# Copies of the gram's blocks on GpSimd, written as products with ones

## The chip, the cores and the metric

The kernel runs on one core of a Trainium2 chip. The metric is device time in microseconds: the median of three runs of the kernel before is 2724.28 us (2723.8 to 2724.82). The core's engines are named in the profile as PE (TensorE matmul) and PEld (its weight loads), DVE (VectorE), ACT (ScalarE), POOL (GpSimd) and SP (SyncE, which only issues DMAs here). They run side by side and wait for each other by semaphores; each executes its own instructions in program order. An instruction that waits holds up everything behind it on its engine.

## The reference, cut to what matters

Eight images of 768 channels and 32x32 pixels pass through two layers, each `x = x + layer(groupnorm(x))`. Layer 0 is an attention whose scores are made of the variances of keys and values. Layer 1 is a 1x1 convolution over the normalised image and 28 correlation channels: the normalised pixel times its neighbours at 28 offsets of a 7x7 window.

```python
def _L1_conv_ref(feature, conv_w, conv_b):
    norm = jnp.sqrt(jnp.sum(feature * feature, axis=1, keepdims=True))
    feat_n = feature / jnp.maximum(norm, EPS)
    feat_pad = jnp.pad(feat_n, ((0, 0), (0, 0), (PAD, PAD), (PAD, PAD)))
    corr = jnp.stack([jnp.sum(feat_pad[:, :, r:h + r, cc:w + cc] * feat_n, axis=1) for r, cc in _offsets()], axis=1)
    x = jnp.concatenate([feature, corr], axis=1)
    out = jnp.einsum('bchw,oc->bohw', x, conv_w) + conv_b[None, :, None, None]
    return out
...
x = x + _L0_conv_ref(_gn(x), L0_conv_W_qkv, L0_conv_W_proj, L0_conv_b_proj)
x = x + _L1_conv_ref(_gn(x), L1_conv_conv_w, L1_conv_conv_b)
```

## The kernel before

All arithmetic is fp32. An image lies on the chip as 128 partitions by 6 channel chunks by 1024 pixels. The large products (keys and values, projection, convolution) use a scheme with seven block products in place of eight; the sums of blocks that it needs for keys and values are made on GpSimd: `make_sums` (lines 584 to 590), eight products or sums of 128x384 (`s`) for each pair of token groups. These are TENSOR_TENSOR instructions.

The order of the work on every engine is written out when the program is built. A planner (`Clock`) keeps an estimated time; jobs get due times with `later.after(...)` and are issued when the estimate reaches them; TensorE's units (a gram, one block product, four steps of attention) are taken from hand-written lists. The estimates fix only the order of instructions; on the chip semaphores alone decide when each starts.

In the main loop, layer 1 of image b-1 runs beside the second half of keys and values and the attention of image b. The attention of a pair of heads goes over 8 key blocks: ScalarE makes the exponentials `ex` (line 721) and, for some pairs, sums of exponentials `junk` (line 731), TensorE multiplies them with the values (`av`, line 746), and ScalarE copies `av` out.

The correlations of layer 1 (class `Corr`) are made from grams. The image `f` has 8 blocks of 128 pixels (4 rows of 32).

- `turn(t)` copies block t into a tile `turn`, in two instructions, the left and the right half of the rows apart (line 1065), each of 128x384 elements in runs of 16. The pool `turnpool` has one buffer. For the last image ScalarE makes these copies (`act_copy`), for the seven others GpSimd.
- `gram(t)` (24 matmuls, line 1080, into `gr`) multiplies the block with the rows about it, and then issues `turn(t + 1)`, which must wait until the gram has read the one buffer. Later VectorE copies `gr` into `win`, and SP stores it.
- After four grams, `diagonals` reads back the wanted diagonals as `dd`. `scale` takes the squared norms `m` on VectorE and raises them to the power -1/2 on GpSimd (`rn`, line 1125, a TENSOR_TENSOR with `ALU.pow`). Five VectorE instructions make `dn` from `dd` and `rn`; TensorE transposes it (`ct`, line 1136), VectorE copies the result to `cr`, and SP stores it. When both halves of the image are stored, `gather` fetches the correlation channels, which the convolution's last units use.

In TensorE's order, the first `ct` of an image stands between 24 and 8 of the 32 `av` matmuls of four attention steps, behind gram 4 and ahead of gram 5 (in the first image, ahead of gram 6 and behind the `av`). On GpSimd, the first `rn` stands behind `turn` 5 and ahead of `turn` 6. `turn` 0 of the images from the second on is issued ahead, between two `make_sums`.

GpSimd has one more kind of work: `spread` takes the largest key variance over all partitions (`most`, line 661, PARTITION_ALL_REDUCE), once for each half of each image's heads. In images two to seven, the one for the first half comes between `turn` 0 and `turn` 1. Instructions named MODIFY_POOL_CONFIG, which are not in the kernel's text, stand before each of these reductions and before some of the products that follow them.

`ones` is a constant tile of 128x64 ones (line 392), there for the attention's column sums. `windows(ap, dims...)` makes a view with steps written out by hand, each as (step, count).

Of the kernel before, what the change touches and what calls it, by code (L numbers as in the profile page):

```python
# [8 lines left out]
ALU = mybir.AluOpType  # L9
# [7 lines left out]
J = C // P  # L17
# [11 lines left out]
HW = W // 2  # L29
# [42 lines left out]
def windows(ap, *dims):  # L72

    return bass.AP(tensor=ap.tensor, offset=ap.offset, ap=[list(d) for d in dims])
# [83 lines left out]
def two_layers(ctx, tc, x, wkv, wproj, bproj, wconv, wcorr, bconv, out):  # L158
    nc = tc.nc
# [53 lines left out]
    def act_copy(us, to, at):  # L213
        nc.scalar.copy(to, at)  # L214
        clock.act = max(clock.act, clock.now) + us
# [175 lines left out]
    ones = const.tile([P, HD], F32, name="ones")  # L391
# [14 lines left out]
    rows = [dconst.tile([NROW, ROW], F32, name=f"rows{i}") for i in range(2)]  # L406
# [642 lines left out]
    class Corr:  # L1049
# [3 lines left out]
        def turn(self, t):  # L1053

            last = self.b == NB - 1
            pl, tag = (expool, "ex") if last else (turnpool, "turn")
            flat = pl.tile([P, N if last else J * P], F32, tag=tag, name=f"turn{self.b}_{t}")[:, : J * P]
            self.turned[t] = flat.rearrange("p (j s m) -> p j s m", j=J, s=2)
            to = flat.rearrange("p (j s y x) -> p j s y x", j=J, s=2, x=HW)
            rows = self.f[:, :, t * P : (t + 1) * P].rearrange("p j (y s x) -> p j y s x", y=4, s=2)  # L1060
            for side in range(2):
                if last:
                    act_copy(0.5, to[:, :, side], rows[:, :, :, side, :])
                else:
                    nc.gpsimd.tensor_copy(to[:, :, side], rows[:, :, :, side, :])  # L1065

        def gram(self, t):

# [440 lines left out]
```

## Time and profile before

The profiled execution took 2723.3 us, of which the core's span in the trace is 2721.6 us; the rest lies around it. TensorE's mean granted clock is 0.992 of full speed.

| | us busy | instructions |
|---|---|---|
| TensorE matmuls | 2649.8 | 9831 |
| VectorE | 1632.4 | 4160 |
| ScalarE | 1365.4 | 1841 |
| GpSimd | 355.3 | 442 |
| of GpSimd: the four lines of `make_sums` | 262.3 | 256 |
| of GpSimd: copies `turn` | 54.5 | 112 |
| of GpSimd: `rn` | 16.5 | 16 |
| of GpSimd: `most` | 6.9 | 16 |

How to read the views. A line of the groups has line, engine, operation, tile written and tile read, count, busy us and mean ns of one, and then the idle time of the engine just before these instructions, with what ended it. A line of the waits has the engine and tile that waited, what it waited for, the us in total, the number of waits and the longest; "issue" stands where the profile shows nothing that was waited for. A line of the view in order of time has start, length, engine, line, operation, tiles and count, and in brackets the idle time before it and its releaser. PEclk is the granted share of TensorE's full clock. Queue entries ("POOLq") are instructions of the engine's sequencer, which are not counted as busy.

### The profile page before, as it was taken

What the parts mean: (1) busy time and instruction counts of PE and PEld (TensorE: products, weight loads), DVE (VectorE), ACT (ScalarE), POOL (GpSimd) and SP (SyncE); (2) the same over time, 40 slices, a digit from 0 to 9 for tenths busy, and PEclk for the clock granted to TensorE, in tenths of its full rate; (3) what the DMA queues carried; (4) which work ended last, traced back from release to release, by engine and by line L of the source; (5) the groups of instructions that cost most, each with busy time, mean ns of one, the idle gap of its engine ahead of it and who ended that gap; (6) DMA issues with size and microseconds to landing.
All of it is one profiled execution on the core that took longest, in us unless ns stands there. A gap on an engine that the chain in (4) does not pass through costs nothing.

```text
span 2721.6 us, 30651 instructions
## 1 busy us (share of the span) xinstructions
PE 2649.8 (97%) x9831; PEld 1230.9 (45%) x9831; DVE 1632.4 (60%) x4160; ACT 1365.4 (50%) x1841; POOL 355.3 (13%) x442
## 2 busy tenths in 40 slices
PE   7999999999999999999999999999999999999999
PEld 4443454345543454434544345443454434544344
DVE  5859734775347853478524875258742587525864
ACT  1497078700697006970079701796017960189600
POOL 4220120003200032000320012200122001220000
PEclk9999999999999999999999999999999999999999
DMA  7764456354553645626556365462654626545243
GB/s 275 297 233 134 142 191 179 105 201 154 158 180 112 205 152 157 194 90 210 158 153 191 92 208 167 141 205 79 223 167 139 189 82 230 172 116 158 86 127 101
DMA packets 323355, 446.04 MB, mean 164 GB/s; under 512 B 59458, under 2 KB 245170, under 8 KB 323194
## 3 DMA queue, kind: packets, MB, share of 16 engines
q1 hardware_dynamic: 321962, 441.32, 50.9%
q10 hardware_dynamic: 1232, 2.75, 0.3%
q8 instruction: 79, 1.29, 0.2%
q14 instruction: 82, 0.67, 0.1%
HBM read 377.49 MB, written 64.40 MB: 162 GB/s over the span
## 4 chain that ended last, share of the span: by engine, by line
PE 89%; DMA 5%; issue 3%; DVE 2%; ACT 1%; POOL 1%; SPq 0%; DVEq 0%; POOLq 0%; ACTq 0%
PE x L359 35%; PE av L746 22%; PE y L359 17%; PE z L359 9%; PE gr L1080 3%; DMA x<-x1d 1%; DMA di<-ir 1%; PE den L779 1%; DMA rd<-di 1%; PE x L988 1%; PE den L829 1%; PE y L988 1%; DMA vdr<-rsv 1%; PE z L988 1%; ACT ex L721 0%
## 5 line engine op out<-in xcount | busy, mean ns | idle before, releaser
L721 ACT ACTIVATE ex<-bc,nk 128x1024 f32<-128x1024 f32 x768 | 826.8, 1137 | 449.1 <-DMA bc<-vdr 227.0
L746 PE MATMUL av<-ex,v 128*64 128x512 f32 x3072 | 705.3, 604 | 4.8 <-ACT ex L721 4.6
L731 ACT ACTIVATE junk<-bk,vm 128x1024 bf16<-128x1024 f32 x368 | 420.4, 1142 | 42.1 <-DMA bk<-kdr 22.8
L746 PEld LDWEIGHTS av<-ex,v 128*64 128x64 f32 x3072 | 230.5, 138 | 442.7 <-issue 380.1
L152 DVE TENSOR_TENSOR acc<-acc,ex 128x1024 f32<-128x1024 f32 x350 | 402.0, 1215 | 0.0
L214 ACT COPY kp<-x 128x384 f32<-128x384 f32 x28 | 13.4, 478 | 559.2 <-PE x L359 559.2
L359 PE MATMUL y<-kv,s 128*128 128x384 f32 x744 | 260.7, 491 | 0.0
L359 PE MATMUL x<-kv,xn 128*128 128x384 f32 x756 | 257.1, 490 | 2.8 <-DVE xn L152 1.6
L359 PE MATMUL x<-kv,s 128*128 128x384 f32 x744 | 254.3, 489 | 0.0
L359 PEld LDWEIGHTS x<-kv,xn 128*128 128x128 f32 x756 | 144.1, 191 | 106.0 <-issue 7.1
L359 PEld LDWEIGHTS x<-kv,s 128*128 128x128 f32 x744 | 138.7, 190 | 101.9 <-issue 9.1
L359 PEld LDWEIGHTS y<-kv,s 128*128 128x128 f32 x744 | 137.8, 190 | 94.8 <-issue 7.3
L480 POOL TENSOR_TENSOR rstda<-vea,neghalf 128x1 f32<-128x1 f32 x8 | 4.8, 595 | 1009.9 <-DVE vea L152 1009.9
L359 PE MATMUL x<-v,wt 128*128 128x512 f32 x288 | 130.2, 596 | 0.0
L359 PE MATMUL z<-kv,xn 128*128 128x384 f32 x372 | 126.9, 488 | 0.0
L152 DVE TENSOR_TENSOR v<-y,v 128x128 f32<-128x128 f32 x180 | 40.9, 282 | 137.5 <-PE y L359 137.5
L359 PE MATMUL x<-f,wt 128*128 128x512 f32 x252 | 116.2, 601 | 1.9 <-DVE x L152 1.8
L584 POOL TENSOR_TENSOR s<-xn 128x384 f32<-128x384 f32 x64 | 68.0, 1070 | 290.2 <-PE x L359 202.2
L152 DVE BATCH_NORM_STATS2 vbn<-v 128x6 f32<-128x64 f32 x720 | 101.8, 211 | 0.0
L152 DVE COPY win<-gr 128x133 f32<-128x133 f32 x64 | 18.4, 288 | 128.2 <-PE gr L1080 118.6
L1065 POOL COPY turn<-f 128x384 f32<-128x384 f32 x112 | 54.5, 514 | 305.4 <-PE gr L1080 292.2
L152 DVE SCALAR_TENSOR_TENSOR x<-x,bconv_sb,x 128x512 f32<-128x512 f32 x63 | 45.8, 746 | 78.1 <-DMA x<-x1d 55.9
(191 smaller groups left out, 3040.3 us busy)
## 6 DMA issues: line engine op xcount, KB each, us to landing
kv<-kvs SPq DMA_DIRECT2D x124, 576.0 KB
kv<-in_wkv_dram SPq DMA_DIRECT2D x95, 576.0 KB
bc<-vdr SPq DMA_DIRECT2D x96, 512.0 KB
f<-in_x_dram SPq DMA_DIRECT2D x48, 512.0 KB
bk<-kdr SPq DMA_DIRECT2D x46, 512.0 KB
x1d<-f SPq DMA_DIRECT2D x42, 512.0 KB
x<-x1d SPq DMA_DIRECT2D x42, 512.0 KB
out_dram<-x SPq DMA_DIRECT2D x82, 256.0 KB
```

Source lines behind the costliest of these rows:

```text
L152: return getattr(self.engine, name)(*args, **kw)
L214: nc.scalar.copy(to, at)
L359: nc.tensor.matmul(t, lhsT=lhsT, rhs=rhs, start=p in FIRST and k == 0, stop=stop and k == len(pairs) - 1, skip_group_check=True,)
L584: nc.gpsimd.tensor_tensor(self.sums[g][:, 0], a[g][2], a[g][3], ALU.add)
L721: nc.scalar.activation(ex, self.bc[e], AF.Exp, scale=self.kv.nk[self.half][:, h, t : t + 1])
L731: nc.scalar.activation(junk, self.bk[e], AF.Exp, scale=self.kv.m2[self.half][:, h, t : t + 1], accum_out=self.sums[:, e, t : t + 1],)
L746: nc.tensor.matmul(self.av[e * HD : (e + 1) * HD, hf, :], lhsT=self.vt[:, t, e, :], rhs=exs[e][:, hf * HF : (hf + 1) * HF], start=t == 0, ...
L779: nc.tensor.matmul(den[at * 32 : (at + 1) * 32, :], lhsT=ones[:, 0:32], rhs=self.acc[e][:, hf * HF : (hf + 1) * HF], start=True, stop=True,)
L829: nc.tensor.matmul(den[e * HD : (e + 1) * HD, :], lhsT=ones, rhs=self.acc[e][:, at], start=True, stop=True)
L988: nc.tensor.matmul(t, lhsT=wcorr_sb[at, i, :], rhs=cs[at, tokens, :], start=False, stop=True, skip_group_check=True)
L1065: nc.gpsimd.tensor_copy(to[:, :, side], rows[:, :, :, side, :])
L1080: nc.tensor.matmul(ps[side * HD : (side + 1) * HD, :n].rearrange("p (y x) -> p y x", x=WIDE), lhsT=block[:, j, side, :], rhs=image[:, 4 * ...
```

## The change

The two GpSimd copies of a `turn` become products of the same block with ones. The second operand is a view of the tile `ones` in which the 6 channel chunks have step 0, the 4 rows a step of 16 and the 16 pixels a step of 1, so that it has the shape of the block. The last image's `turn`, on ScalarE, stays as it is.

```diff
@@ -1062,7 +1062,8 @@
                 if last:
                     act_copy(0.5, to[:, :, side], rows[:, :, :, side, :])
                 else:
-                    nc.gpsimd.tensor_copy(to[:, :, side], rows[:, :, :, side, :])
+                    half = rows[:, :, :, side, :]
+                    nc.gpsimd.tensor_tensor(to[:, :, side], half, windows(ones, ones.ap[0], (0, J), (HW, 4), (1, HW)), ALU.mult)
```

Lines behind it are one higher in the changed kernel: `rn` is line 1126 there, `ct` 1137, the gram 1081.

## The prediction

> **What bounds the kernel now.** I read the page first, then the waits of TensorE, VectorE and GpSimd, then each of these engines in order of time around the longest waits.
>
> ```profile
> PE 2649.8 (97%) x9831; PEld 1230.9 (45%) x9831; DVE 1632.4 (60%) x4160; ACT 1365.4 (50%) x1841; POOL 355.3 (13%) x442
> ...
> L584 POOL TENSOR_TENSOR s<-xn 128x384 f32<-128x384 f32 x64 | 68.0, 1070 | 290.2 <-PE x L359 202.2
> ...
> L1065 POOL COPY turn<-f 128x384 f32<-128x384 f32 x112 | 54.5, 514 | 305.4 <-PE gr L1080 292.2
> ```
>
> TensorE has work for 97% of the span; GpSimd, whose instructions change, for 13%. A saving can only come from TensorE's 72 us without work (2721.6 - 2649.8) or from slow matmuls. The last two lines are the prices: a product of 128x384 takes twice a copy of the same size. Next the waits, from one answer for all engines: us in total, times, longest.
>
> ```profile
> DVE dn L152 <- POOL rn L1125: 57.4, 8, 9.7
> ...
> POOL rn L1125 <- issue: 45.5, 6, 8.2
> ...
> PE ct L1136 <- DVE dn L152: 33.4, 6, 6.2
> ```
>
> Nearly half of TensorE's idle time is one wait, six times: the transpose `ct` of the normalised diagonals waits for `dn`, VectorE for `rn`, and GpSimd, six times, waits before `rn` for nothing that the profile names. The view of line 1125 names what stands there:
>
> ```profile
> L1125 POOLq MODIFY_POOL_CONFIG  x12: 11/11/11, 722.6 to 2400.7; - x12
> ```
>
> Two such instructions precede each of the six `rn`, one for each image from the second to the seventh that goes through layer 1 beside the next image's attention. GpSimd in order of time in the first of these six:
>
> ```profile
> 683.90 0.43 POOL L661 PARTITION_ALL_REDUCE most<-top  x1 [7.43 <-DVE top L152]
> 688.71 0.95 POOL L1065 COPY turn<-f 128x384 f32<-128x384 f32 x2 [4.37 <-PE gr L1080]
> ...
> 721.59 0.96 POOL L1065 COPY turn<-f 128x384 f32<-128x384 f32 x2 [8.49 <-PE gr L1080]
> 730.46 1.05 POOL L1125 TENSOR_TENSOR rn<-m,neghalf 128x4 f32<-128x4 f32 x1 [7.92 <-issue]
> ```
>
> The reduction over partitions (`most`) needs one loaded set of GpSimd functions, a product another. Copies run under either: those of `turn` follow `most` with no change. So the change back waits for the first product, `rn`, and comes when `rn` is urgent: its operand `m` is ready at 722.1, the last copy at 722.5, and `rn` starts at 730.46. TensorE there:
>
> ```profile
> 721.27 5.32 PE L746 MATMUL av<-ex,v 128*64 128x512 f32 x24
> 732.49 0.41 PE L1136 MATMUL ct<-ident,dn 128*80 128x128 f32 x1 [5.90 <-DVE dn L152]
> 732.83 3.19 PE L746 MATMUL av<-ex,v 128*64 128x512 f32 x8
> 735.86 1.53 PE L1080 MATMUL gr<-f,turn 128*64 128x133 f32 x24
> ...
> 748.60 7.04 PE L746 MATMUL av<-ex,v 128*64 128x512 f32 x32
> ```
>
> And the table by stretches; behind the busy times stand PEclk, the DMA share and GB/s:
>
> ```profile
> 732.50:735.90 3.40, 3.40 (x11) 1.06 (x13) 0.28 (x1) 0.00 (x0) 0.00 (x0) 0.57 0.10 27
> 748.60:755.40 6.80, 6.80 (x36) 2.30 (x34) 0.55 (x2) 4.88 (x6) 0.95 (x2) 1.00 0.35 123
> ```
>
> After the 5.9 us without work the clock granted to TensorE is 0.57 instead of 1.00, and 8 `av` matmuls take 3.0 us, where later 32 take 6.87. The wait costs more than its own length.
>
> **What the Trainium skill says.** "GPSIMD Engine Reference", 2.1 Instruction dispatch: the first call of a freshly loaded GpSimd kernel also pays some 6 us of loading, with no visible profile instruction. The trace agrees in kind: 7.17 to 8.22 us in the six places. The trace adds that loading does not wait for the first call: where the next product has long to wait (`rstda` at 611.27), it starts 0.09 us after VectorE's `vea` ends at 611.18. The same page, 4.1 Engine selection, puts one-input work on GpSimd near line rate and two-input work far below it; the two price rows above agree. "TensorE: Matmul & The Clock Gate", Part 1: after about 3.4 us without work the matmul clock falls to half, and stays there until some 3.4 us of work have passed; this is the 0.57.
>
> **The change part by part.**
>
> (a) All 112 copies (2 halves x 8 blocks x 7 images) become products with `ones`. Price: the pairs of existing products take 1.95 to 1.97 us where a pair of copies takes 0.95; so +1.0 us for each of 56 `turn`s. The 16-element runs of this pattern are not shown for a product: bounds +0 and, say, +2 us a pair; I take +1.0, since the copy has the same runs.
>
> (b) Where copies ran under the reduction's functions, the first product now forces the change back. Comparing the instruction order of the two kernels on GpSimd, the pair of change instructions leaves its place before `rn` and stands directly behind `most`, ahead of `turn` 1, in the same six images. Nothing else moves on any engine; the number of changes is the same.
>
> What (b) removes. Counted from start to start, a warm `av` matmul takes 6.87/32 = 0.215 us, and `ct` passes in 0.24 (402.02 to 402.26 in the first image, which has no such wait). So `gr` 5 could start at 721.27 + 24 x 0.215 + 0.24 + 8 x 0.215 = 728.38 instead of 735.86: 7.48 us, of which about 6 are the wait and 1.4 the slow clock. The other five, read alike: 6.94, 8.71, 7.44, 6.92, 7.74 (in the third and sixth `gr` 5 itself also takes 0.5 longer, included). Sum 45.2 us.
>
> What is late next: the product `turn` 5 is released at 721.59 and ends at 723.55; `rn` (1.05) ends at 724.6; the five `dn` instructions take 0.85, so `dn` is ready at about 725.5, and TensorE reaches `ct` at 726.4. Margin 0.9 us. The `ex` for the 8 `av` behind it is ready at 725.4, needed at 726.7. ScalarE then copies `av` out: it waits 6.36 us there today, so it gains some 6.3, and at 750.52 it waits 1.99 us for TensorE, where it catches up the rest. TensorE, ScalarE, VectorE and the SP queue behind `cr` all start earlier by the same amount, and the loads used in the next 20 us were issued by 718. I expect the gain to last to the end.
>
> What (b) adds. The loading starts when `most` ends, 684.33, takes 7.2 to 8.2 us (mean 45.5/6 = 7.6), and `turn` 1 follows with 1.97: done at 693.5 to 694.5. `gr` 1 starts today at 694.67 (10.34 us after `most`; 10.35 in the third of the six). Cost 0, taking a longest load 0.1; if loading beside other traffic took 9 us, 0.7 x 6 = 4 us. Queued behind it are only `turn` 2 onward, whose grams are 5.9 us or more from their release; `turn` 0 and the sums `s` come before. The sums behind `turn` 6 come 1 us later relative to TensorE; the first is used 2.8 us after its end.
>
> What (a) adds on the path. TensorE waits for `turn` once today, at the first gram of the first image (361.7, 2.91 us): the second half now arrives 1.0 us later. There also `turn` 2 (released 372.11) ends at 374.08, with its gram at 374.04: 0.1. Elsewhere in the six images the spacing hides it.
>
> Sum: -45.2 + 1.0 + 0.1 = -44.1. The profiled execution took 2723.3 (span 2721.6) and would take 2679.2; the runs' median, 2724.28, stands 1.0 above it: 2680.2, so 2680.
>
> **The rivals.**
>
> Rival 1, the loading spoils the grams: it starts late (only when `turn` 1 is released, 688.71) or lasts long, so `turn` 1 ends near 688.7 + 7.6 + 2.0 = 698.3 and `gr` 1 is 3.6 us late in six images, perhaps with a short slow clock: 22 to 33 back, 2702 to 2713. Against it: `rstda` shows an early start. For it: the memory traffic at this place differs. 8%.
>
> Rival 2, part of the gain is absorbed downstream by DMAs or ScalarE, which is without a gap from 752 to 800: say a third to a half, 2695 to 2702. Against it: ScalarE's waits for TensorE before and after. 9%.
>
> Rival 3, slower: the product in this pattern is very slow on GpSimd, by its 16-element runs with two inputs. At D us for one, `gr` 1 is late by 2D - 2.7 us in six images (684.33 + 7.6 + 2D against 694.67); from D = 5.0, 6 x 7.3 = 44, the gain is gone, somewhat earlier because beyond D = 2.9 later grams are late too. At D = 6 it is about 2745. Existing products take 1.0. 3%.
>
> That the order doesn't change as compared is the rest of "no change": 1%.
>
> **How the numbers follow.** My case, 79%, with 2676 to 2692 its own range: the unknown loading time (4), the pattern's price (up to 2.6 for each of six if the pair takes 4 us), and a few us more where VectorE, now free of 57.4 us of waiting, hands over something earlier. Rivals 1 and 2 lie just above; I take 2676 to 2696, which leaves out under 2 in 10. A measurement here tells 0.2%, about 5 us, from no change. Faster: 79 + 8 + 9 = 96%; same 1%; slower 3%.
>
> **What would show it.** The wait of `ct` for `dn` gone; the wait "issue" before `rn` gone and one of about 3 us before `turn` 1 in its place; `turn` rows of 1.0 us; PEclk 1.00 in the stretch after `ct`; `gr` waiting for `turn` about 4 us in total. `gr` waiting six times for several us means rival 1; unchanged TensorE idle time with new wait lines, rival 2; `turn` above 2 us, rival 3.

## The result, and the profile after

The changed kernel takes 2679.2 us (median of 4 runs, 2678.51 to 2681.84) against 2724.04 us of the kernel before (4 runs): ratio 0.9841, 95% interval 0.9823 to 0.9858, so 39 to 48 us less. The prediction said 2680. The profiled execution took 2678.86 us, its span 2677.1 us; 44.4 us less than that of the kernel before.

The page and the groups of the changed kernel:

```profile
PE 2637.3 (99%) x9831; PEld 1230.4 (46%) x9831; DVE 1637.2 (61%) x4160; ACT 1364.2 (51%) x1841; POOL 411.7 (15%) x442
...
L1066 POOL TENSOR_TENSOR turn<-f,ones 128x384 f32<-128x384 f32 x112 | 111.6, 1017 | 265.9 <-PE gr L1081 207.5 <-issue 30.9 <-PE ptk L538 14.3
```

GpSimd has more to do: 411.7 us of work instead of 355.3, and the increase is that of `turn` (111.6 instead of 54.5). TensorE's idle time (span less busy) fell from 71.8 to 39.8 us, and its busy time, for the same 9831 records, by 12.5 us. (A record is not a matmul of the text here: `gram` issues 12 matmuls and has 24 records in the trace, and the four steps of attention issue 16 and have 32. All counts of matmuls taken from views, the 24 and 32 above too, are of records.)

The waits of the changed kernel, from one answer for all engines:

```profile
POOL turn L1066 <- issue: 30.9, 4, 7.9
...
DVE dn L152 <- POOL rn L1126: 15.9, 8, 2.8
POOL turn L1066 <- PE ptk L538: 14.3, 2, 7.2
...
PE gr L1081 <- POOL turn L1066: 4.0, 2, 3.5
```

The wait of `ct` for `dn` is gone from TensorE's list, and `rn` no longer waits for "issue". The six waits for the loading now stand before `turn` 1: four named "issue", two put down to a matmul (`ptk`) that had ended about 0.6 us before. They need 45 us, as before, but nobody waits for them. GpSimd and then TensorE in order of time, in the first of the six images:

```profile
685.01 0.43 POOL L661 PARTITION_ALL_REDUCE most<-top  x1 [7.42 <-DVE top L152]
693.34 1.97 POOL L1066 TENSOR_TENSOR turn<-f,ones 128x384 f32<-128x384 f32 x2 [7.90 <-issue]
...
722.71 1.97 POOL L1066 TENSOR_TENSOR turn<-f,ones 128x384 f32<-128x384 f32 x2 [7.47 <-PE gr L1081]
724.64 1.06 POOL L1126 TENSOR_TENSOR rn<-m,neghalf 128x4 f32<-128x4 f32 x1
```

```profile
695.78 1.58 PE L1081 MATMUL gr<-f,turn 128*64 128x133 f32 x24
...
722.38 5.32 PE L746 MATMUL av<-ex,v 128*64 128x512 f32 x24
727.63 0.31 PE L1137 MATMUL ct<-ident,dn 128*80 128x128 f32 x1
727.87 1.94 PE L746 MATMUL av<-ex,v 128*64 128x512 f32 x8
729.64 1.53 PE L1081 MATMUL gr<-f,turn 128*64 128x133 f32 x24
```

The two MODIFY_POOL_CONFIG entries stand at the end of `most` (685.44), and `turn` 1 ends at 695.31, 0.47 us ahead of gram 1 at 695.78. `rn` follows `turn` 5 without a gap, and TensorE passes `ct` without one. From the start of the 24 `av` to gram 5 it takes 7.26 us; before it took 14.59.

### The profile page after: what moved, and what is told of

The parts are those of the page before. It is cut to its first block, busy times and chain, and to the rows that moved or that the text cites. A ratio compares the mean times of both kernels' runs of the same rounds, so it can differ in the third digit from the quotient of the medians.

```text
span 2677.1 us, 30651 instructions
## 1 busy us (share of the span) xinstructions
PE 2637.3 (99%) x9831; PEld 1230.4 (46%) x9831; DVE 1637.2 (61%) x4160; ACT 1364.2 (51%) x1841; POOL 411.7 (15%) x442
## 4 chain that ended last, share of the span: by engine, by line
PE 92%; DMA 4%; DVE 2%; issue 1%; ACT 0%; SPq 0%; POOL 0%; DVEq 0%; POOLq 0%; ACTq 0%
PE x L359 36%; PE av L746 24%; PE y L359 17%; PE z L359 9%; PE gr L1081 3%; DMA x<-x1d 1%; PE den L779 1%; PE x L988 1%; PE den L829 1%; PE y L988 1%; DMA di<-ir 1%; PE z L988 1%; DMA rd<-di 1%; DMA vdr<-rsv 0%; DMA x1d<-f 0%
## 5 line engine op out<-in xcount | busy, mean ns | idle before, releaser
L721 ACT ACTIVATE ex<-bc,nk 128x1024 f32<-128x1024 f32 x768 | 826.3, 1137 | 444.8 <-DMA bc<-vdr 173.9
L746 PE MATMUL av<-ex,v 128*64 128x512 f32 x3072 | 694.3, 596 | 4.9 <-ACT ex L721 4.7
L1066 POOL TENSOR_TENSOR turn<-f,ones 128x384 f32<-128x384 f32 x112 | 111.6, 1017 | 265.9 <-PE gr L1081 207.5
L359 PEld LDWEIGHTS z<-kv,xn 128*128 128x128 f32 x372 | 69.9, 190 | 49.2 <-issue 2.3
```

The source lines that it names most:

```text
L359: nc.tensor.matmul(t, lhsT=lhsT, rhs=rhs, start=p in FIRST and k == 0, stop=stop and k == len(pairs) - 1, skip_group_check=True,)
L721: nc.scalar.activation(ex, self.bc[e], AF.Exp, scale=self.kv.nk[self.half][:, h, t : t + 1])
L746: nc.tensor.matmul(self.av[e * HD : (e + 1) * HD, hf, :], lhsT=self.vt[:, t, e, :], rhs=exs[e][:, hf * HF : (hf + 1) * HF], start=t == 0, ...
L1066: nc.gpsimd.tensor_tensor(to[:, :, side], half, windows(ones, ones.ap[0], (0, J), (HW, 4), (1, HW)), ALU.mult)
```

## The experiments

All ratios are to the kernel before on the same chip.

**One product in place of 112.** Is it the place of the loading, or that products replace copies?

```diff
                 if last:
                     act_copy(0.5, to[:, :, side], rows[:, :, :, side, :])
+                elif t == 1 and side == 0 and self.b:
+                    half = rows[:, :, :, side, :]
+                    nc.gpsimd.tensor_tensor(to[:, :, side], half, windows(ones, ones.ap[0], (0, J), (HW, 4), (1, HW)), ALU.mult)
                 else:
                     nc.gpsimd.tensor_copy(to[:, :, side], rows[:, :, :, side, :])
```

> Six products instead of 112: only the left half of turn 1, in images two to seven, is a product with ones; every other copy stays a copy. Theory (the place of the loading decides): the loading again stands directly behind most, so ct waits for dn no more and the matmuls behind ct run at full clock: 45 us less than the kernel before, 2679 us or a ratio of 0.983 to 0.985, and about 1 us less than the changed kernel in the profile, since turn 0 of the first image stays a copy. Rival (products as such help, as copies slow something else on the chip): the gain goes with the number of products, 6 of 112, so 2722 us. Rival (the loading spoils gram 1): TensorE waits for turn 1 six times.

Measured: 2677.59 us, ratio 0.9832 (0.9817 to 0.9846). In the trace `ct` waits in none of the six images. Six products bring the whole gain; the other 106 bring nothing.

**Products everywhere but there.** The opposite: 52 products, and turns 1 to 5 of images two to seven stay copies.

```diff
-                else:
+                elif t in (0, 6, 7) or not self.b:
+                    half = rows[:, :, :, side, :]
+                    nc.gpsimd.tensor_tensor(to[:, :, side], half, windows(ones, ones.ap[0], (0, J), (HW, 4), (1, HW)), ALU.mult)
+                else:
                     nc.gpsimd.tensor_copy(to[:, :, side], rows[:, :, :, side, :])
```

> 52 products: all of the first image's turns, and turns 0, 6 and 7 of images two to seven; turns 1 to 5 of these stay copies, so that the first product behind most is rn again. Theory: the loading stays before rn, the six waits of ct for dn come back with 33 us in all and the slow clock behind them; nothing is gained, and 1 us is lost at the first gram: 2725 us, ratio 1.000. Rival (products as such help): 52 of 112 of the gain, 2703 us.

Measured: 2724.89 us, ratio 1.0009 (1.0001 to 1.0018). Its waits:

```profile
POOL rn L1128 <- issue: 43.6, 6, 7.6
...
PE ct L1139 <- DVE dn L152: 31.5, 6, 5.6
```

The loading is back before `rn`, and so is the wait of `ct`. With the run before, this settles the first question: products in place of copies are worth nothing where they do not move the loading.

**A product that does nothing but load.** All copies stay; a product of 128x1 elements stands behind `most`.

```diff
             nc.gpsimd.partition_all_reduce(most, top, P, bass_isa.ReduceOp.max)
+            if half == 0 and b > 1:
+                tiny = st.tile([P, 1], F32, tag="tiny", name=f"tiny{b}")
+                nc.gpsimd.tensor_tensor(tiny, neghalf[:, 0:1], neghalf[:, 0:1], ALU.mult)
```

> All copies stay copies; one extra product of 128x1 elements is put directly behind most in images two to seven, with no use but to bring the loading there. Theory: the whole gain without any of the price: 2678 us, ratio 0.983; the six ct waits gone, turn 1 waits for the loading (7 to 8 us behind most) and ends 1 us further ahead of gram 1 than in the changed kernel; the first gram waits 2.9 us, as before. Rival (products as such help): no gain, 2724 us.

Measured: 2677.39 us, ratio 0.9834 (0.9817 to 0.985), in order of time on GpSimd:

```profile
681.86 0.43 POOL L661 PARTITION_ALL_REDUCE most<-top  x1 [7.42 <-DVE top L152]
689.73 0.18 POOL L664 TENSOR_TENSOR tiny<-neghalf 128x1 f32<-128x1 f32 x1 [7.43 <-issue]
689.87 0.94 POOL L1068 COPY turn<-f 128x384 f32<-128x384 f32 x2
```

The loading has its own instruction now, and the copies behind it keep their old length. `turn` 1 ends at 690.81, 1.8 us ahead of gram 1 (692.64), where the changed kernel has 0.47.

**The product further back.** The same 128x1 product, behind `turn` 4 instead of `most`.

```diff
                 else:
                     nc.gpsimd.tensor_copy(to[:, :, side], rows[:, :, :, side, :])
+            if t == 4 and 0 < self.b < NB - 1:
+                tiny = st.tile([P, 1], F32, tag="tiny", name=f"tiny{self.b}")
+                nc.gpsimd.tensor_tensor(tiny, neghalf[:, 0:1], neghalf[:, 0:1], ALU.mult)
```

> All copies stay copies; the 128x1 product that brings the loading stands behind turn 4 in images two to seven, not behind most. The loading then runs from about 712 to 720 in the first of these (times of the kernel before), where turn 5 is released at 721.6. Theory (any place with 8 us free ahead of rn does): the same gain as with the product behind most, 2678 us, ratio 0.983. Rival (it must be behind most, or a load beside other traffic takes longer than there): turn 5 and rn are late, ct waits again, up to 2 us in each of six: 2690 us.

Measured: 2678.77 us, ratio 0.9832 (0.9816 to 0.9849). Its waits:

```profile
POOL tiny L1068 <- issue: 50.1, 6, 9.8
...
DVE dn L152 <- POOL rn L1128: 13.5, 8, 3.2
```

The loads took longer here (50.1 us in six instead of 45), and `dn` once waited 3.2 us for `rn`, but TensorE waited for `dn` at none of the six `ct`. Nothing is special about the place behind `most`: what counts is some 8 us, here up to 10, in which nobody needs GpSimd, ahead of `rn`.

**Filling the wait.** Does the wait cost more than its length, by the matmul clock? In the kernel before, TensorE gets unused matmuls ahead of `ct`, whose result `ct` overwrites; the loading stays where it was.

```diff
                 pt = small(f"ct{b}_{hf}")
+                if hf == 0 and 0 < b < NB - 1:
+                    for n in range(11):
+                        nc.tensor.matmul(pt, lhsT=ident, rhs=self.f[:, 0, 0:HF], start=True, stop=True)
```

> The kernel before with 11 unused matmuls of 128x512 put ahead of ct in the six images (some 4.7 us of TensorE work, overwritten by ct), so that TensorE is busy during most of the wait; the loading stays before rn. Theory (the wait costs its length and then the slow clock): ct starts when it did, at the mercy of rn, but PEclk behind it is 1.00, the 8 av matmuls behind ct take 1.7 instead of 3 us, and 10.8 us of the 45 come back: 2713 us, ratio 0.996. Rival (the matmuls behind ct are slow for another reason, or the trace only models them so): no change, 2724 us.

Measured: 2733.05 us, ratio 1.0039 (1.0024 to 1.0054): slower by 11 us. The number was missed because the size of the filling was: each of these matmuls stands in the trace as two records, start to start about 0.43 us, and the estimate had counted one.

```profile
724.54 9.71 PE L1138 MATMUL ct<-f,ident 128*128 128x512 f32 x22
734.09 0.27 PE L1139 MATMUL ct<-ident,dn 128*80 128x128 f32 x1
734.29 1.94 PE L746 MATMUL av<-ex,v 128*64 128x512 f32 x8
```

The filling took 9.55 us (724.54 to 734.09), longer than the wait. Even so it says something: six times 9.55 are 57.3 us added. Had the filling replaced the waits alone (some 34 us, counted from where `ct` could have started), the kernel would have lost 23; against waits and slow clock together (45.2) it would lose 12. It lost 11 (6.5 to 14.7). The run was repeated with 5 matmuls:

> As the filled wait, but with 5 unused matmuls ahead of ct in place of 11: with the 0.87 us that each took there, 4.3 us of work in a wait of 5.3 to 6.2 us. Theory (wait plus slow clock): ct still starts when rn lets it, about 1 to 2 us after the last unused matmul, and finds the full clock; 10.8 us come back: 2713 us against 2724, ratio 0.996. Rival (no cost of the clock beyond the wait itself): 2724 us.

Measured: 2710.7 us, ratio 0.9948 (0.9933 to 0.9963), 10 to 18 us less than the kernel before, by doing unused work. TensorE in order of time, and the table by stretches (PEclk is the third number from the end):

```profile
724.41 4.56 PE L1138 MATMUL ct<-f,ident 128*128 128x512 f32 x10
730.20 0.31 PE L1139 MATMUL ct<-ident,dn 128*80 128x128 f32 x1 [1.23 <-DVE dn L152]
730.43 1.94 PE L746 MATMUL av<-ex,v 128*64 128x512 f32 x8
```

```profile
724.00:733.00 9.00, 7.77 (x38) 3.36 (x36) 1.09 (x6) 4.19 (x8) 1.05 (x1) 1.00 0.33 102
```

`ct` still comes when `rn` lets it; only the 1.23 us behind the filling are idle, PEclk stays 1.00, and the 8 `av` take 1.94 us by the trace instead of 3.19. So the slow clock was a cost of its own. In the trace, the time from `most` of the second image to the end is 11.4 us shorter than before, about a quarter of the gain of the changed kernel; the runs, with 10 to 18 us, are no finer than that.

**Products twice.** How close is the changed kernel to paying for its longer `turn`?

```diff
-                    nc.gpsimd.tensor_tensor(to[:, :, side], half, windows(ones, ones.ap[0], (0, J), (HW, 4), (1, HW)), ALU.mult)
+                    for again in range(2):
+                        nc.gpsimd.tensor_tensor(to[:, :, side], half, windows(ones, ones.ap[0], (0, J), (HW, 4), (1, HW)), ALU.mult)
```

> The changed kernel with every product of a turn done twice into the same place (224 products), so that a turn takes 3.9 us in place of 1.97. Theory, from the margins in the profile of the changed kernel: turn 1 (load included) now ends after gram 1's turn on TensorE, by 1.46, 1.15, 0.66, 0.75, 1.37 and 1.26 us in the six images, 6.7 in all; turn 5 pushes rn back by 1.95 us, so that ct waits about 1 us in each, 5.8 in all; the first image's first and third gram lose 3.9. Together 16: 2695 us. Rival (the time of the products is hidden whatever it is): 2679 us.

Measured: 2698.9 us, ratio 0.9906 (0.9891 to 0.9921), well behind the changed kernel's 0.9841. In the profile it is 18.6 us slower than the changed kernel (span 2695.7 against 2677.1); 16.4 were expected.

```profile
PE gr L1082 <- POOL turn L1067: 11.9, 10, 4.5
...
PE ct L1138 <- DVE dn L152: 7.0, 6, 1.2
```

Both margins are as small as they were read: with `turn` some 2 us longer, grams and `ct` wait again. A doubled `turn` takes 4.15 us, 2.18 more instead of the 1.95 that were reckoned with. That shows at `ct`, where the six images lose 7.2 us from the 24 `av` to gram 5 instead of 5.8, and in the first image, which loses 4.7 up to gram 4 instead of 3.9. These two are the 2.2 us by which the forecast was short; the rest (6.2 us in the six images, where 6.7 were expected at gram 1, and 0.4 elsewhere) nearly cancels out.

## Why the prediction was right

*The cause.* That the loading moves from before `rn` to behind `most`, and that this alone carries the gain, is shown from both sides: six products or a 128x1 product there bring it all, 52 products elsewhere nothing. That a set of functions is loaded in this time is not shown: the traces have the MODIFY_POOL_CONFIG entries and 7 to 8 us behind them in which GpSimd starts nothing, and that this is a load is taken from the section that the prediction cites for it ("GPSIMD Engine Reference" of the Trainium skill, 2.1 Instruction dispatch).

*The size of the gain.* 45.2 us were forecast. From `most` of the second image to the end of the span the kernel before takes 2721.6 - 683.90 = 2037.7 us, the changed one 2677.1 - 685.01 = 1992.1: 45.6 less. At the six places themselves, from the 24 `av` to gram 5 and counting in the two grams that ran slow before, it is 44.3: the term was 0.9 us too large, as a stretch without a wait takes 7.26 us and not the 7.11 that were reckoned. The rest, a little over 1 us, fell elsewhere and is no more than the spread of the kernel itself: from one image's `most` to the next the changed kernel takes 327.6 to 328.8 us. The part for the slow clock, which the "TensorE: Matmul & The Clock Gate" page of the Trainium skill (Part 1) suggested and the table by stretches showed, was needed: without it the forecast would have been 11 us short. The half filled wait shows it apart.

*What is late next.* Forecast: `dn` ready 0.9 us before TensorE reaches `ct`. It is ready at 726.54 (the last `dn` ends), `ct` starts at 727.63, with no wait. The products done twice took the margin and made `ct` wait.

*The load on the way to gram 1.* Forecast: 7.2 to 8.2 us and no cost. The six loads took from 7.1 to 7.9 us, and `turn` 1 ended 0.5 to 1.3 us ahead of gram 1. Rival 1 fell, narrowly. That loading starts at once and not with the first product, read from `rstda`, holds: `turn` 1 is released only at the end of gram 0, 689.7, and starts 3.6 us later, half of the shortest of the six loads, but 7.9 us after `most`. For the same reason the wait before `turn` 1 reads 7.1 to 7.9 us in the view, and not about 3 as the prediction's list of signs has it: the view counts from the end of `most`.

*No loss downstream.* Rival 2 fell: the 45.6 us stand at the end of the span.

*The price of a product.* 1.0 us forecast, 1.017 measured (mean of 112). The rows that the prediction calls existing products are the sums and differences of `make_sums`; that a multiplication costs the same, and needs the same set, was assumed, and came out so. (Its "far below" for work with two inputs is a factor of 2 here: 1017 ns against 514 for a copy.) Rival 3, that the 16-element runs make it slow, fell.

*The term that was most mis-sized* is the first gram of the first image: +1.0 us forecast, +2.7 measured (from the start of `turn` 0 to gram 1: 361.16 to 370.23 before, 361.65 to 373.42 after). Its wait grew from 2.91 to 3.46 and 0.52 us, about as forecast, but the matmuls behind it now ran at a lower clock:

```profile
361.72 1.92 PE L1080 MATMUL gr<-f,turn 128*64 128x133 f32 x23 [2.91 <-POOL turn L1065]
```

```profile
362.72 0.44 PE L1081 MATMUL gr<-f,turn 128*64 128x133 f32 x2 [3.46 <-POOL turn L1066]
363.68 2.41 PE L1081 MATMUL gr<-f,turn 128*64 128x133 f32 x21 [0.52 <-POOL turn L1066]
```

The same stretch, 364.5 to 368.0, in the kernel before and in the changed one:

```profile
364.50:368.00 3.50, 3.50 (x19) 2.26 (x17) 0.85 (x7) 3.50 (x5) 0.34 (x1) 1.00 0.07 20
```

```profile
364.50:368.00 3.50, 3.50 (x23) 2.74 (x21) 1.44 (x9) 1.45 (x4) 1.54 (x2) 0.58 0.01 3
```

PEclk is 1.00 before and 0.58 after. The 52 products elsewhere, which make the same first `turn`s, lose the same 2.7 us there; every version in which these stay copies loses nothing. The price that was put on the slow clock behind the six long waits was not put on this short one. In the sum it didn't show, and that is luck: between 449 and 487 us TensorE waits a few times for ScalarE's exponentials, and 8 `av` there took 4.56 us in the profiled execution of before and 2.97 in that of after; the whole stretch was 2.1 us shorter. That stretch varies by itself, whichever part of the change a run carries: behind the same wait of 2.79 us the 8 `av` took 4.72 us with one product (first line) and 2.97 us with the 128x1 product behind `most` (second line).

```profile
480.27 4.72 PE L746 MATMUL av<-ex,v 128*64 128x512 f32 x8 [2.79 <-ACT ex L721]
```

```profile
481.21 2.97 PE L749 MATMUL av<-ex,v 128*64 128x512 f32 x8 [2.79 <-ACT ex L724]
```

So the 2.1 us are no effect of the change, and nearly cancelled the loss at the first gram.

Whether the versions with a 128x1 product or a single product are faster than the changed kernel can't be told: their ratios are 0.9832 to 0.9834 against 0.9841, with intervals that overlap, and the traces show 2.7 us less at the first gram, less than these intervals are wide.

## What to carry to other kernels

An instruction whose function set is not loaded pays for the load where it stands in its engine's order, not where the set was displaced; when one engine alternates between two sets, look for the place of the reload and put any instruction of the needed set, however small, where that engine has time. Busy time on a mostly idle engine says little: here GpSimd's work grew by 56 us and the kernel gained 45. A wait of TensorE is to be priced with the slow matmuls behind it. The waits of 5 to 6 us had them every time, those of about 3 us only sometimes, so a short wait is worth keeping from growing.

## What the runs showed of the hardware

- A plain copy on GpSimd runs under the functions that the reduction over partitions needs; a product does not. In the six images the load was 6.9 to 8.5 us in all nine profiled executions, but for one of 9.85 (behind `turn` 4, fifth of the six). Before the first `most` of the program, where the reduction's functions come in, it was 9.1 to 10.9 us in eight of the nine, and at most 7.9 in the kernel before; why is open. "GPSIMD Engine Reference" of the Trainium skill, 2.1 Instruction dispatch, gives about 6 us; the measured figure is the one to use.
- A start on GpSimd is not decided by semaphores alone: in the kernel before, `rn` started 7.9 us after its operand was ready and its engine free.
- A product of 128x1 elements takes 0.18 us, the power of 128x4 elements 1.03 us.
- About 1 us more of waiting, from 2.9 to 4.0 us in two pieces, brought the clock from 1.00 to 0.58 over 3.5 us of the work behind it. A fixed limit does not come out of the runs: the same wait of 2.79 us for `ex` was followed by slow `av` in two executions and by fast ones in four.
